# Two-layer graph network on one core: second-step products moved ahead of the attention, last normalization spread over other engines

## The chip, the core and the metric

The kernel runs on one core of a Trainium2 chip (trn2). The core has a matrix engine (TensorE; PE in the profile, with PEld for its weight loads), VectorE (DVE), ScalarE (ACT), GpSimd (POOL), and SyncE (SP), which here only issues DMAs. Each engine runs its own instructions in order and waits for the others through semaphores. Matrix products land in PSUM, everything else lies in SBUF or in DRAM. The metric is the device time of one execution in microseconds; the time before is the median of 3 runs.

## What is computed

Layer 0 is a graph attention layer with four heads over 4096 nodes; the change doesn't touch it. Layer 1 works on X = relu(layernorm(x)), 4096 rows of 256, in f32:

```
R = (S + I) / row sums                  # S: the adjacency matrix
Z = 0; Xf = X; Xa = X
for n in range(2):
    A  = top_p_attention(Xa)            # softmax of q k^T, cut to the top 90%, divided by its row sums
    Xf = R @ Xf
    Xa = A @ Xa
    Z  = Z + Xf @ U1[n].T + Xa @ U2[n].T
h = X + Z
out = x + (layernorm(h) * ln_g + ln_b)
```

q and k are products of Xa with 64-wide weights. The two parts that matter here are `Xa @ U2[n].T` and the closing layernorm.

## The kernel before

The 4096 rows are 32 blocks of 128 rows (P = 128, NB = 32). Layer 0 runs until about 830 us. Then each of the two steps has the same stages.

**A hop with the keys.** `hops` forms R @ Xf (line 601), 256 pieces of 4 products each, streaming the adjacency matrix from DRAM. It is a generator; between its pieces the kernel takes one item of `fills` and one of `picks`, two further generators. `fills` begins with `projections`: for each group g of 4 blocks it transposes 4 blocks of `cur` (line 732) into `xs`, multiplies xs with the merged key and query weights (line 738), and transposes the result into kT and qT (line 743). Each `yield` in `projections` is a place where the hop goes on. `fills` and `picks` then do the logits, exponentials and cuts of blocks 0 to 2. R @ Xf leaves in transposed form to `xft_d`, in step 0 also by rows to `xf_d`. In step 1 `cur` is loaded from `xa_d`, where step 0 left A @ Xa.

**The blocks.** For b = 0 to 31, `chosen_kept(b)` places the work of VectorE and GpSimd, and `attend` that of TensorE and ScalarE. In program order `chosen_kept(b)` has: `candidates(b)` (VectorE, many MAX8), `finish_scale(b-3)`, `first_step(b+2)` (some twenty small GpSimd instructions, lines 885 to 914, which end in the bound c), `third_probe(b+1)` (VectorE, one pass of 4096 columns, line 929, needs c), `finish(b-2)`, `finish_rows(b-3)`, and `masked(b)` (VectorE, one pass, line 972, gives the cut matrix e and its scale). `attend(b)` then works on block b while it makes the logits and exponentials of block b+3, called `ahead`:

- `start(c)`: a logits group, 4 products (line 701), and its exponentials on ScalarE (line 861), for c = 0 to 3
- `turn(g)`: 4 transposes of e (line 1035) into one of two PSUM tiles `tp`, and a copy to `eT` on ScalarE (line 1037); `gather(g)`: 4 products of eT with cur into `acc` (line 1043), g = 0 to 7
- `contribute(before)` and `contributed(before)`: for the block before, the row block xa is transposed (line 1055), copied to `zT` (line 1057), and multiplied with U2; the block's R @ Xf, `xf`, is multiplied with U1 (all four products in line 1063)
- `summed` and `first_probe` on ScalarE (lines 874 to 879 and 868), two passes per half of e
- `scaled`: A @ Xa out of acc, times the row scale (line 1047), to `xa_d` in step 0

So the order on TensorE at the start of a block is: logits 0, transposes of the block before's xa, turn 0, logits 1, turn 1, four products with U1 and U2, gather 0, logits 2, and so on. In the last three blocks of a step there is no block ahead and so no logits. In block 30, `looked` counts rows to be repaired (a small product, line 829, after the last cut); the repair itself stands in a branch behind each step.

**The end of a block.** `finish` adds the U1 part times rinv, the U2 part and, in step 0, X, in step 1 the partial sum z; step 0 stores to `z_d`, step 1 takes mean and variance (lines 148, 149). In step 1 `finish_scale` adds ln_b to x1 (line 1226) and computes 1/sqrt(variance + eps) on GpSimd (lines 1228, 1229), `finish_rows` does three VectorE passes of 256 columns (1233 to 1235) and SyncE stores the rows (1236).

**Weights.** `weights(n)` asks for U1[n] and U2[n] on SyncE's queue after the hop (line 691). `l1e` is a pool of four large tiles (tag e1), which hold the matrices e of the blocks and, in `projections`, kq and xs.

The order of calls is written out by hand (`manual_schedule`); each engine keeps it.

Of the kernel before, what the change touches and what calls it, by code (L numbers as in the profile page):

```python
# [26 lines left out]
P = 128  # L27
# [29 lines left out]
def gat_then_top_p_diffusion(  # L57
# [57 lines left out]
    z_d = dram.tile([NB, P, D], F32, name="z_d")  # L115
    x1_d = dram.tile([NB, P, D], F32, name="x1_d")
# [569 lines left out]
    def weights(n):  # L686

        both = l1.tile([P, 2, KC, D], F32, name="u")
        S.u = [both[:, i] for i in range(2)]
        for t, u in zip(S.u, (u1_t, u2_t)):  # L690
            nc.sync.dma_start(t, u[n].rearrange("(k p) m -> p k m", p=P))
# [23 lines left out]
    def projections(cur, n, G):  # L715
# [10 lines left out]
        lengths = small.tile([P, NB, 2], F32, name="lengths", bufs=1)  # L726
        for g in range(NB // 4):
# [6 lines left out]
            yield from waits(1 + n)  # L734
            pm = ps2.tile([P, 2, 512], F32, name="mm")
# [5 lines left out]
            yield from waits(1 + n)  # L741
# [9 lines left out]
            yield from waits(1 + n)  # L751
# [96 lines left out]
    def began(n, b, G):  # L848
# [6 lines left out]
        r.sums = small.tile([P, 2, 4], F32, name="sums", bufs=6)  # L855
        return r
# [166 lines left out]
    def loads(r):  # L1023
        r.xf, r.part = rows.tile([P, KC, P], F32, name="xf"), rows.tile([P, D], F32, name="part", bufs=3)
        nc.sync.dma_start(r.xf, xft_d[r.n][ds(r.b, 1)].rearrange("o p s i -> (o p) s i"))
        if r.n > 0:
            nc.sync.dma_start(r.part, block(z_d, r.b))
            r.x1 = rows.tile([P, D], F32, name="x1", bufs=3)
            nc.sync.dma_start(r.x1, block(x1_d, r.b))
        r.acc = ps1.tile([P, 2, D], F32, name="acc")  # L1030

# [13 lines left out]
    def scaled(r):  # L1045
        r.xa = rows.tile([P, D], F32, name="xa")
        nc.scalar.activation(r.xa, r.acc[:, 0, :], AF.Copy, scale=r.scale)
        if r.n + 1 < STEPS:
            nc.sync.dma_start(block(xa_d, r.b), r.xa)

    def contribute(r):

        pt = ps2.tile([P, 4, P], F32, name="tp")
        for k in range(KC):
            nc.tensor.transpose(pt[:, k, :], r.xa[:, ts(k, P)], ident)
        zT = rows.tile([P, 4, P], F32, name="eT", bufs=3)
        nc.scalar.copy(zT[:, :KC], pt[:, :KC])  # L1057
        return zT

    def contributed(r, zT):  # L1060
        for i, t in ((1, r.xf), (0, zT)):
            for k in range(KC):
                nc.tensor.matmul(r.acc[:, i, :], t[:, k, :], S.u[1 - i][:, k, :], start=(k == 0), stop=(k == KC - 1))  # L1063

    def attend(r, cur, before, ahead, between={}, eT=()):
# [8 lines left out]
        zT = contribute(before) if before else None  # L1074
        loads(r)
        eT = list(eT) or [turn(r, 0)]
        start(1)
        for g in range(NB // 4):
            if g + 1 < NB // 4:
                eT.append(turn(r, g + 1))  # L1080
            if g == 0 and before:
                contributed(before, zT)
            gather(r, eT[g], g, cur)
            if g < 2:
# [5 lines left out]
            if g in between:  # L1090
                between[g]()
        scaled(r)
# [85 lines left out]
    def completed(R, cur):  # L1178
# [6 lines left out]
        if r.n + 1 < STEPS:  # L1185
            r.x = rows.tile([P, D], F32, name="a_x", tag="xa")
            nc.vector.tensor_copy(r.x, X[:, ds(dve, 1), :].rearrange("p o d -> p (o d)"))
# [6 lines left out]
        contributed(r, contribute(r))  # L1194
        finish(r)
        finish_scale(r)
        finish_rows(r)
# [12 lines left out]
    def finish(r):  # L1210

        if r.n + 1 < STEPS:
            row, ri = (r.x, r.ri) if hasattr(r, "x") else (X[:, r.b, :], rinv[:, r.b:r.b + 1])
            nc.vector.scalar_tensor_tensor(r.part, r.acc[:, 1, :], ri, row, ALU.mult, ALU.add)
            nc.vector.tensor_add(r.part, r.acc[:, 0, :], r.part)
            nc.sync.dma_start(block(z_d, r.b), r.part)
        else:
            ri = r.ri if hasattr(r, "ri") else rinv[:, r.b:r.b + 1]
# [177 lines left out]
```

## Time and profile before

| | |
|---|---|
| median of 3 runs | 2915.61 us (2913.66 to 2918.56) |
| the profiled execution | 2918.28 us; its span 2916.5 us |
| granted TensorE clock, mean | 0.988 |
| hop of step 1 with the second keys | about 1866 to 2168 us |
| blocks of step 1 | about 2168 to 2906 us |
| VectorE busy, 1170 to 1840 us (step 0) | 575.80 of 670 us |
| VectorE busy, 2215 to 2880 us (step 1) | 636.38 of 665 us |
| ScalarE busy in the same stretches | 500.82 and 482.91 us |
| GpSimd busy in the same stretches | 194.30 and 308.63 us |
| products of line 1063 | 512 instructions, 131.6 us busy |
| transposes of line 1055 | 128 instructions, 24.8 us busy |

A row of the profile's groups names line, engine, operation, and the tiles as out<-in. PE MATMUL times are modelled and overlap, so the distance between the starts of successive instructions says more than the duration of one. An f32 product appears as two instructions. In a timeline each row is one run of like instructions: start, length, engine, line, and in brackets the idle time before it with what ended it.

### The profile page before, as it was taken

What the parts mean: (1) busy time and instruction counts of PE and PEld (TensorE: products, weight loads), DVE (VectorE), ACT (ScalarE), POOL (GpSimd) and SP (SyncE); (2) the same over time, 40 slices, a digit from 0 to 9 for tenths busy, and PEclk for the clock granted to TensorE, in tenths of its full rate; (3) what the DMA queues carried; (4) which work ended last, traced back from release to release, by engine and by line L of the source; (5) the groups of instructions that cost most, each with busy time, mean ns of one, the idle gap of its engine ahead of it and who ended that gap; (6) DMA issues with size and microseconds to landing.
All of it is one profiled execution on the core that took longest, in us unless ns stands there. A gap on an engine that the chain in (4) does not pass through costs nothing. (4 is left out here: it accounts for less than half of the span.)

```text
span 2916.5 us, 51977 instructions
## 1 busy us (share of the span) xinstructions
PE 2828.3 (97%) x19033; PEld 2475.8 (85%) x19033; DVE 2196.8 (75%) x5193; ACT 1908.9 (65%) x3063; POOL 763.6 (26%) x1661
## 2 busy tenths in 40 slices
PE   6899999999999999999999999999999999999998
PEld 4799999999977778888888888788778888888887
DVE  7776878778654384788888888442747999999996
ACT  6786787768633735777777776235337777777772
POOL 6501211111010210233322222000103444444442
PEclk8899999999999999999999999999999999999999
DMA  7969577695465784000000000488970000000000
GB/s 178 220 244 219 194 218 189 231 201 205 157 196 166 248 299 135 20 24 22 20 20 20 20 20 21 153 270 280 337 268 22 25 25 25 25 25 30 29 23 22
DMA packets 181148, 368.12 MB, mean 126 GB/s; under 512 B 17168, under 2 KB 133904, under 8 KB 176784
## 3 DMA queue, kind: packets, MB, share of 16 engines
q1 hardware_dynamic: 142352, 270.92, 28.2%
q0 software_dynamic: 21504, 83.89, 12.1%
q10 hardware_dynamic: 17024, 9.85, 1.1%
q8 instruction: 154, 2.52, 0.4%
q14 instruction: 114, 0.93, 0.1%
HBM read 301.35 MB, written 109.38 MB: 141 GB/s over the span
## 5 line engine op out<-in xcount | busy, mean ns | idle before, releaser
L1043 PE MATMUL acc<-X,eT 128*128 128x256 f32 x4096 | 966.0, 381 | 0.1
L1043 PEld LDWEIGHTS acc<-X,eT 128*128 128x128 f32 x4096 | 743.2, 190 | 97.7 <-ACT eT L1037 14.9
L391 PE MATMUL acc<-ut,m 128*128 128x195 bf16 (+1 forms) x8192 | 700.9, 247 | 8.2 <-DVE st L408 5.6
L391 PEld LDWEIGHTS <-m 128*128 128x128 fp8e4 x8192 | 696.4, 97 | 13.2 <-DVE st L408 4.7
L861 ACT ACTIVATE e<-mm,nm 128x1024 f32<-128x1024 f32 x256 | 287.0, 1121 | 311.0 <-PE mm L701 295.7
L365 ACT ACTIVATE g<-sr,d_big 128x1024 uint8<-128x1024 f32 x444 | 467.7, 1139 | 2.6 <-DVE m L371 2.6
L929 DVE SCALAR_TENSOR_TENSOR big<-e,c 128x4096 f32<-128x4096 f32 x58 | 273.0, 4707 | 121.2 <-POOL c L914 84.4
L1037 ACT COPY eT<-tp 128x512 f32<-128x512 f32 x512 | 299.6, 585 | 98.3 <-PE tp L1035 97.9
L885 POOL TENSOR_TENSOR sums<-sums 128x2 f32<-128x2 f32 x64 | 12.5, 196 | 1309.0 <-ACT void L868 1309.0
L947 DVE MAX8 cand<-big 128x8 f32<-128x228 f32 (+1 forms) x1152 | 348.3, 380 | 0.0
L601 PE MATMUL mm<-ar,hl 128*128 128x512 f32 x844 | 336.3, 401 | 10.8 <-DMA ar<-adj_d 2.9
L601 PE MATMUL acc<-ar,hl 128*128 128x512 f32 x844 | 329.4, 393 | 1.5 <-DVE ar L588 1.4
L1035 PE MATMUL tp<-ident,e 128*128 128x128 f32 x2048 | 310.5, 274 | 2.7 <-ACT eT L1057 0.3
L1035 PEld LDWEIGHTS tp<-ident,e 128*128 128x128 f32 x2048 | 248.7, 141 | 70.9 <-ACT eT L1057 28.4
L371 DVE TENSOR_TENSOR m<-g,ax 128x512 uint32<-128x512 uint32 x256 | 182.2, 712 | 115.5 <-PE acc L391 96.3
L972 DVE SCALAR_TENSOR_TENSOR e<-e,found 128x4096 f32<-128x4096 f32 x58 | 259.6, 4476 | 0.0
L868 ACT ACTIVATE void<-e,c1x 128x2048 int8<-128x2048 f32 x128 | 257.4, 2011 | 2.8 <-issue 2.0
L868 ACT ACTIVATE void<-e,c 128x2048 int8<-128x2048 f32 x128 | 257.4, 2011 | 0.0
L701 PE MATMUL mm<-kT,qT 128*128 128x512 f32 x512 | 197.6, 467 | 3.6 <-ACT e L861 2.2
L601 PEld LDWEIGHTS mm<-ar,hl 128*128 128x128 f32 x844 | 159.4, 189 | 48.6 <-issue 5.9
L372 DVE TENSOR_TENSOR m<-m,ax 128x512 uint32<-128x512 uint32 x256 | 177.7, 694 | 26.0 <-DVE m L371 0.9
L601 PEld LDWEIGHTS acc<-ar,hl 128*128 128x128 f32 x844 | 159.6, 189 | 34.5 <-DVE ar L588 2.6
(297 smaller groups left out, 3494.6 us busy)
## 6 DMA issues: line engine op xcount, KB each, us to landing
ar<-adj_d SPq DMA_DIRECT2D x211, 512.0 KB, 4.7
adj_d<-ax POOLq DMA_DIRECT2D x32, 2048.0 KB, 6.9
ut<-uv_d SPq DMA_DIRECT2D x60, 784.0 KB, 5.4
aru<-adj_d SPq DMA_DIRECT2D x45, 512.0 KB, 4.6
ax<-in_adj_t_dram POOLq DMA_DIRECT2D x32, 512.0 KB, 15.7
x<-xf_d SPq DMA_DIRECT2D x78, 128.0 KB, 5.1
xf<-xft_d SPq DMA_DIRECT2D x64, 128.0 KB, 2.2
sr<-s_d SPq DMA_DIRECT2D x15, 512.0 KB, 4.7
```

The costliest lines, as they stand in the source:

```text
L365: nc.scalar.activation(g[:, c, :], shared[k].sr, AF.Relu, scale=BIG, bias=d_big[:, h, j:j + 1])
L391: nc.tensor.matmul(shared[k].acc[i][:, t, :cols], m[t][:, c, ts(i, P)], shared[k].ut[j // QUARTER][:, j % QUARTER, t, :cols], start=(j == ...
L601: nc.tensor.matmul(A.acc[c][s], A.hl[m][:, t, ts(s, P)], A.ar[m][:, ts(c, 512)], start=(j == 0 and t == 0), stop=(j == NB - 1 and t == 1))
L701: nc.tensor.matmul(pm[:, h, :], q[t], kT[:, ds(h * (N // 2) + c * 512, 512)], start=(t == 0), stop=(t == 1))
L861: nc.scalar.activation(ev[:, :, c, :], r.pm[c], AF.Exp, bias=r.nm, accum_out=r.sums[:, c // 2, c % 2:c % 2 + 1])
L868: nc.scalar.activation(void, r.e[:, ts(h, N // 2)], (AF.Relu, AF.Sign)[i], bias=r.c1, scale=-1.0, accum_out=r.sums[:, h, 2 + i:3 + i])
L929: nc.vector.scalar_tensor_tensor(big, r.e, r.c3, r.e, ALU.is_le, ALU.mult, accum_out=r.low3)
L947: nc.vector.max(cand[:, s, :], big[:, edges[s]:edges[s + 1]])
L972: nc.vector.scalar_tensor_tensor(r.e, r.e, r.t, r.e, ALU.is_ge, ALU.mult, accum_out=kept)
L1035: nc.tensor.transpose(pt[:, i, :], r.e[:, ts(4 * g + i, P)], ident)
L1037: nc.scalar.copy(eT, pt)
L1043: nc.tensor.matmul(r.acc[:, 0, :], eT[:, i, :], cur[:, j, :], start=(j == 0), stop=(j == NB - 1))
```

## The change

- In step 1 `carried` multiplies each block's rows of Xa, while the keys are made, with U2 of both steps side by side (one product 512 wide for each half of the 256 inputs). The half for U2[0] is stored to a new DRAM tensor `v_d`; the half for U2[1] replaces the block's rows in `cur`. Since A @ (Xa @ U2.T) is (A @ Xa) @ U2.T, `gather` of step 1 then yields the U2[1] part itself.
- `contribute` is gone, and `contributed` holds only the two U1 products, at the end of the block's own `attend` (in block 31 of step 1 after gather 4, into a bank of its own).
- `weighed` copies that product, times rinv, to SBUF on ScalarE; `gathered` adds z, v and ln_b on GpSimd; `finish` of step 1 becomes one VectorE pass and the moments; `normal` (ScalarE) and `polished` (GpSimd) replace the three VectorE passes for all but the last two blocks, where `finish_rows` has two passes.
- In `chosen_kept` the GpSimd order is now polished(b-3), finish_scale(b-2), first_step(b+2), gathered(b-1).
- U2 is asked for in the last block of step 0 (`both_weights`, a tile of pool l1e), U1 after the hop as before.

```diff
+    def both_weights():
+        u2 = l1e.tile([P, N + NB], F32, name="u2", tag="e1")[:, :KC * STEPS * D].rearrange("p (k n m) -> p k n m", k=KC, n=STEPS)
+        for i in range(STEPS):
+            nc.sync.dma_start(u2[:, :, i, :], u2_t[i].rearrange("(k p) m -> p k m", p=P))
+        S.u2 = [u2]
...
+        def carried(xs, g, i):
+            if n == 0:
+                return
+            b = 4 * g + i
+            pt = ps2.tile([P, 4, P], F32, name="tp").rearrange("p a b -> p (a b)")
+            for k in range(KC):
+                nc.tensor.matmul(pt, xs[:, k, i, :], u2[:, k].rearrange("p n m -> p (n m)"), start=(k == 0), stop=(k == KC - 1))
+            v = rows.tile([P, D], F32, name="part", bufs=3)
+            nc.scalar.copy(v, pt[:, :D])
+            nc.scalar.dma_start(block(v_d, b), v)
+            nc.vector.tensor_copy(cur[:, b, :], pt[:, D:])
...
             yield from waits(1 + n)
+            carried(xs, g, 0)
             pm = ps2.tile([P, 2, 512], F32, name="mm")
...
-            yield from waits(1 + n)
+            yield
+            carried(xs, g, 1)
+            yield from waits(n)
...
-            yield from waits(1 + n)
+            yield
+            carried(xs, g, 2)
+            yield from waits(n)
+            carried(xs, g, 3)
+            if n > 0:
+                yield
...
     def scaled(r):
-        r.xa = rows.tile([P, D], F32, name="xa")
-        nc.scalar.activation(r.xa, r.acc[:, 0, :], AF.Copy, scale=r.scale)
         if r.n + 1 < STEPS:
...
-    def contributed(r, zT):
-        for i, t in ((1, r.xf), (0, zT)):
-            for k in range(KC):
-                nc.tensor.matmul(r.acc[:, i, :], t[:, k, :], S.u[1 - i][:, k, :], start=(k == 0), stop=(k == KC - 1))
+    def contributed(r):
+        for k in range(KC):
+            nc.tensor.matmul(r.far, r.xf[:, k, :], S.u1[:, k, :], start=(k == 0), stop=(k == KC - 1))
+
+    def weighed(r):
+        if r.n + 1 == STEPS:
+            nc.scalar.activation(r.xf.rearrange("p k i -> p (k i)"), r.far, AF.Copy, scale=r.ri)
+
+    def gathered(r):
+        if r.n + 1 == STEPS:
+            nc.gpsimd.tensor_tensor(r.part, r.part, r.v, ALU.add)
+            nc.gpsimd.tensor_tensor(r.x1, r.x1, ln_b_r, ALU.add)
+            nc.gpsimd.tensor_tensor(r.part, r.part, r.xf.rearrange("p k i -> p (k i)"), ALU.add)
...
+        if not last:
+            contributed(r)
+            weighed(r)
         scaled(r)
...
         else:
-            ri = r.ri if hasattr(r, "ri") else rinv[:, r.b:r.b + 1]
-            nc.vector.scalar_tensor_tensor(r.part, r.acc[:, 1, :], ri, r.part, ALU.mult, ALU.add)
-            nc.vector.tensor_add(r.part, r.acc[:, 0, :], r.part)
+            nc.vector.scalar_tensor_tensor(r.part, r.acc[:, 0, :], r.scale, r.part, ALU.mult, ALU.add)
...
+    def normal(r):
+        if r.n + 1 == STEPS:
+            nc.scalar.activation(r.part, r.part, AF.Identity, scale=r.rs, bias=r.nmr)
+
+    def polished(r):
+        if r.n + 1 == STEPS:
+            nc.gpsimd.tensor_tensor(r.part, r.part, ln_g_r, ALU.mult)
+            nc.gpsimd.tensor_tensor(r.part, r.part, r.x1, ALU.add)
+            nc.sync.dma_start(block(out.rearrange("(b p) d -> b p d", p=P), r.b), r.part)
...
                 if b > 2:
-                    finish_scale(blocks[b - 3])
-                if b + 2 < NB and not hasattr(blocks[b + 2], "stepped"):
-                    first_step(blocks[b + 2])
+                    polished(blocks.pop(b - 3))
...
                 if b > 1:
                     finish(blocks[b - 2])
-                if b > 2:
-                    finish_rows(blocks.pop(b - 3))
+                    finish_scale(blocks[b - 2])
+                if b + 2 < NB and not hasattr(blocks[b + 2], "stepped"):
+                    first_step(blocks[b + 2])
+                if 0 < b < NB - 1:
+                    gathered(blocks[b - 1])
                 if not hasattr(r, "kept"):
                     masked(r)
+                if 1 < b < NB - 1:
+                    normal(blocks[b - 2])
```

## The prediction

> **What bounds the kernel now.** I read the page first: its busy row and its chain of waits.
>
> ```profile
> PE 2828.3 (97%) x19033; PEld 2475.8 (85%) x19033; DVE 2196.8 (75%) x5193; ACT 1908.9 (65%) x3063; POOL 763.6 (26%) x1661
> ...
> PE acc L1043 12%; PE mm L701 4%; PE acc L601 3%; PE mm L601 3%; PE tp L1035 3%; ACT void L868 2%; PE acc L1063 2%; DVE e L972 0%; DMA X<-xa_d 0%; DMA ar<-adj_d 0%; PE mm L738 0%; ACT eT L1037 0%; DVE cand L947 0%; ACT e L861 0%; PE tp L732 0%
> ```
>
> TensorE leads the chain, but 97% is an average over stages. So I cut the span into stretches. The change touches three: the blocks of step 0 (about 1123 to 1862 us), the second hop with the second keys (1866 to 2168), and the blocks of step 1 (2168 to 2906). For the hop I asked for stretches of 20 us (columns: busy us with counts for PE, PEld, DVE, ACT, POOL; granted clock; DMA share; GB/s):
>
> ```profile
> 1900.00:1920.00 20.00, 19.84 (x120) 17.29 (x120) 11.01 (x20) 8.34 (x19) 0.00 (x0) 1.00 0.93 307
> 1920.00:1940.00 20.00, 20.00 (x125) 17.56 (x124) 10.00 (x19) 6.92 (x15) 0.00 (x0) 1.00 0.92 304
> ```
>
> While the keys are made PE has no gap to fill: work added there is paid in full, and the loads (DMA 0.93) only become more relaxed. For the blocks I read the timeline where one block ends and the next begins (step 0):
>
> ```profile
> 1402.93 0.41 PEld L701 LDWEIGHTS mm<-kT,qT 128*128 128x128 f32 x2
> ...
> 1403.87 0.33 PEld L1055 LDWEIGHTS tp<-ident,xa 128*128 128x128 f32 x2
> ...
> 1404.32 1.12 ACT L861 ACTIVATE e<-mm,nm 128x1024 f32<-128x1024 f32 x1 [0.50 <-PE mm L701]
> ...
> 1405.42 0.36 ACT L1057 COPY eT<-tp 128x256 f32<-128x256 f32 x1
> ...
> 1405.68 0.60 ACT L1037 COPY eT<-tp 128x512 f32<-128x512 f32 x1
> 1405.84 0.42 PEld L1035 LDWEIGHTS tp<-ident,e 128*128 128x128 f32 x4 [0.48 <-ACT eT L1057]
> ...
> 1406.23 0.73 PEld L1063 LDWEIGHTS acc<-u,xf 128*128 128x128 f32 x4
> ...
> 1406.99 0.84 PEld L1063 LDWEIGHTS acc<-u,eT 128*128 128x128 f32 x4
> ...
> 1407.85 1.70 PEld L1043 LDWEIGHTS acc<-X,eT 128*128 128x128 f32 x8
> ```
>
> I call 1402.93 the join, J: the last gather is out and the next block's work starts. The first gather starts at J+4.92 (1407.85). Between them lie two logits groups, two turns, the two transposes of L1055, the four products of L1063, and one stall of 0.48 us, for which the copy L1057 is named. A block lasts 23.35 us in both steps (the chain's x16 gather pieces in step 1 stand at 2466.08, 2489.43, 2512.77).
>
> **Part 1, the joins.** The change takes L1055, L1057 and the U2 half of L1063 away, and puts the two U1 products at the block's end, before the next logits. Removing 0.33 + 0.86 + 0.48 would suggest 1.6 us, but the transposes behind L1055 and behind the stall run in 0.43 and 0.42 us against 0.55 elsewhere. I therefore add up PE's new order by starts: U1 products 0.86, logits 0.94, turn 0.55, logits 0.77, turn 0.55 = J+3.67. That is a gain of 1.25 if nothing else is late. What is late next is ACT: in the trace the exponentials (L861) start 1.39 us after their logits' weights, the next copy can start 1.10 later, and the copy L1037 takes 0.60. The logits now start at J+0.86, so the first eT is there at 0.86 + 1.39 + 1.10 + 0.60 = J+3.95, and the gather starts at J+4.00. PE waits 0.33 us in a new place and the join gains 0.92 us. In step 1 ACT also gets L1047's successor (weighed, 0.48) once the U1 products are out, and one normal (about 0.41, as the 128x256 casts of L578): both end near J+2.1, just ahead of the exponentials at J+2.25. After the first gather nothing of PE's and ACT's order changes. There are 31 joins in each of 2 steps: 62 x 0.92 = **57 us gained**. The last three joins of a step have no logits and would gain 1.3 to 1.6, but there the totals of L829 wait for VectorE (PE already waits 1.5 us at 2881.8), so I leave them at 0.92.
>
> **Part 2, the products with both U2.** carried() adds, for each of 32 blocks of step 1, two products of 128x512 in f32. Each f32 product is two instructions (4096 of L1043 for 2048 products). No f32 product of that width is in the trace. By width the nearest row is L601 (f32r, one every 0.23 us); by type it is the gather, 256 wide:
>
> ```profile
> 2900.08 1.89 PE L1043 MATMUL acc<-X,eT 128*128 128x256 f32 x8
> ...
> 2902.25 3.62 PE L1043 MATMUL acc<-X,eT 128*128 128x256 f32 x16
> ```
>
> Eight more instructions take 1.73 us: 0.216 each for 256 columns. The Trainium skill (TensorE: Matmul & The Clock Gate, Back-to-back issue gap) gives N/2.4 + 2.5 ns, so 109 ns for 256 columns and 216 ns for 512. The row is twice the rule: an f32 instruction streams at half the pace, and I double with the width. By the rule the part would cost 32 x 4 x 0.216 = 28 us, by the row 32 x 4 x 0.43 = **55 us added**. I take the row, since its type is the same; 28 stays as the lower end. Above, change-overs and a late tile could add some 4 us. The two evacuations of each (ACT 0.37, DVE 0.42) and the store on ACT's queue lie under PE: ACT is busy 7 to 8 and DVE 10 to 11 of 20 us there. If that cover failed, carried() would wait for its PSUM tile, of which there are two. The eight more pauses in the generator shift the later picks by 8 of 256 pieces, about 9 us; the last pick ended at 2146, 22 us before the hop did. The early request of U2 is worth nothing: nothing waits for L690 now.
>
> **Part 3, ends.** At the end of step 0 the hop's products wait from 1861.28 to 1864.05 (2.77 us) for the last contribution; only the U1 products, 0.86, remain: 1.9 gained. At the very end the last gather's weights are in at 2905.46 and the last VectorE instruction ends at 2912.58, 7.1 later. New: acc is read 0.45 later (0.48), statistics 0.46 and 0.27, POOL 0.22 + 0.09 + 0.56 with the first fused pass beside it, last pass 0.43, plus some 0.4 because the two share a port: 3.4. That is **3.7 gained**.
>
> **Part 4, normalization.** In step 1 VectorE loses L1220 (0.45 from start to start) and three passes for which ACT and POOL stand in (1.22): its round, 23.23 us now (2499.84 to 2523.07, no gap), falls to 21.56. GpSimd gets three additions after first_step (gathered), two before it (polished) and one small instruction, less one addition: about 0.73 us each. Now the rule that speaks against it: the skill (SBUF — State Buffer, the single rule of the shared port pair) says a VectorE instruction with two SBUF inputs and a GpSimd instruction that reads SBUF exclude each other, whoever is second being fully blocked. The timeline agrees:
>
> ```profile
> 2499.77 0.73 POOL L1226 TENSOR_TENSOR x<-x,ln_b_r 128x256 f32<-128x256 f32 x1
> ...
> 2499.84 4.94 DVE L929 SCALAR_TENSOR_TENSOR big<-e,c 128x4096 f32<-128x4096 f32 x1 [0.16 <-POOL c L911]
> ...
> 2500.59 4.27 POOL L1228 TENSOR_SCALAR rs<-mv 128x1 f32<-128x1 f32 x1
> ```
>
> L929 took 4.94 instead of 4.49 us behind an addition, and a 0.2 us instruction took 4.27 behind L929. By the rule alone a blocked VectorE pass loses the whole 0.73, by the row 0.46; I use 0.46. If VectorE starts L929 the moment c is ready (J+7.2), one gathered addition passes with it (in the 21.56), two wait for its end and hold up finish: 1.46; polished hits L972: 0.46. That makes 23.5, more than the new block of 22.43. But then VectorE falls behind TensorE, c no longer releases L929, and the additions run ahead of it; 1.5 us behind, the round is about 22.0. There is room: L972 ends at J+19.3 now, near J+20 then, and the turn needs it at J+24. The other new waits also fit: SP's store of the output now waits for POOL's polished at about J+15, where it is issued today (2507.57), so swapped and loads behind it keep their time; normal in ACT's queue needs finish_scale by J+24 with the exponentials behind it, and finish_scale comes near J+21; first_step behind finish_scale on POOL is wanted at J+22.8. I cost this part at nothing.
>
> **Sum.** -57 + 55 - 1.9 - 3.7 = -7.6 us. The profiled execution took 2918.28 (span 2916.5 and 1.8 around it) and would take 2910.7; it lay 2.7 above the median of the three runs, 2915.61. Forecast: **2908 us**.
>
> **Rivals.** (A) The sum as above, chance 0.45, 2902 to 2913. (B) More is gained, chance 0.30: the wide product costs less than doubled (down to 28 us: 2881), or eT is not late at the join (62 x 1.25 = 78 gained: 2888). For it: the widths were extrapolated. Against: the f32 rows all pace at two cycles a column, and ACT's chain is read from the trace. (C) Slower, chance 0.13: the shared port makes VectorE the bound of step 1. It decides once contention costs more than 22.43 - 21.1 = 1.3 us a block at any lag; at 23.5 us a block, 28 blocks lose 1.07 each, 30 us: 2938. For it: L1228's 4.27 us. Against: the lag heals it. (D) Chance 0.12: PE in the hop also waits for carried's tiles, 0.1 to 0.4 us each, 3 to 13 us: 2911 to 2921. That the work merely moves from the blocks to the hop without effect lies between A and D.
>
> **Chances and range.** A measurement of this kernel can tell about 0.2%, 5.8 us: faster means below 2909.8. A gives 0.31 faster and 0.14 same; B 0.30 faster; C 0.09 slower, 0.04 same; D 0.07 same, 0.05 slower. That is 0.61, 0.25, 0.14. The range runs from B's 2884 to D's 2921 and leaves out most of C.
>
> **What would show it.** Joins: the time from the end of the last gather to the first gather falls from 4.92 to 4.0, with a wait of 0.3 for eT (L1037's copy) and a block of 22.4 in both steps. Hop: the new row 128x512 f32 x128 at 0.43 us apart, and a hop some 55 us longer. Step 1: POOL rows of 4 us beside L929 and L972, VectorE full, but no PE wait on L972. I am wrong if blocks of step 1 are longer than those of step 0 (C), if the products pace at 0.22 (B), or if PE waits on tp tiles in the hop (D).

## The result and the profile after

| | before | after |
|---|---|---|
| median | 2915.61 us (2913.66 to 2918.56) | 2897.87 us (2896.88 to 2900.28) |
| ratio | | 0.9941, 95% interval 0.9928 to 0.9954 |
| profiled execution, its span | 2918.28, 2916.5 us | 2899.5, 2897.7 us |
| block of step 0, of step 1 (first gather to first gather) | 23.35, 23.35 us | 22.31, 22.25 us |
| last gather's end to first gather, regular joins | 4.96, 4.96 us | 4.02, 3.97 us |
| first gather to first gather of the last block: step 0, step 1 | 719.2, 718.2 us | 686.2, 687.2 us |
| hop with the second keys: step 0's last gather to step 1's first | 309.6 us | 357.0 us |
| first gather of step 1's last block to the end | 27.5 us | 25.1 us |

The change made the kernel 17.7 us faster; 2908 was forecast. In the rows below, line numbers are those of the changed kernel: gather L1075 (was L1043), logits L707 (L701), turn L1067 and its copy L1069 (L1035, L1037), exponentials L890 (L861), third probe L958 (L929), masked L1001 (L972), hop products L602 (L601), U1 products L1085, products with both U2 L741.

The page of the changed kernel, its busy row, its chain of waits, and two of its groups:

```profile
PE 2814.0 (97%) x18777; PEld 2443.1 (84%) x18777; DVE 2171.2 (75%) x5069; ACT 1914.8 (66%) x3061; POOL 878.6 (30%) x1815
...
DVE 18%; PE 11%; issue 5%; DMA 2%; ACT 1%; POOL 0%; SPq 0%; ACTq 0%; DVEq 0%; POOLq 0%
...
L1085 PE MATMUL acc<-u,xf 128*128 128x256 f32 x252 | 64.9, 380 | 0.4
...
L741 PE MATMUL tp<-u,xs 128*128 128x512 f32 x128 | 60.5, 595 | 0.0
```

The chain now names VectorE ahead of TensorE. That invites the reading that VectorE has become the bound; the experiments below say otherwise.

The timeline of the changed kernel at a join of step 0 (start, length, engine, line; in brackets the idle time and what ended it):

```profile
1413.40 0.84 PEld L1085 LDWEIGHTS acc<-u,xf 128*128 128x128 f32 x4
...
1414.26 0.41 PEld L707 LDWEIGHTS mm<-kT,qT 128*128 128x128 f32 x2
...
1415.66 1.12 ACT L890 ACTIVATE e<-mm,nm 128x1024 f32<-128x1024 f32 x1 [0.52 <-PE mm L707]
...
1416.77 0.57 ACT L1069 COPY eT<-tp 128x512 f32<-128x512 f32 x1
...
1417.39 1.59 PEld L1075 LDWEIGHTS acc<-X,eT 128*128 128x128 f32 x8 [0.25 <-ACT eT L1069]
```

J is 1413.40. The logits start at J+0.86, the exponentials 1.40 later, the copy 1.11 after those, and the gather at J+3.99, as soon as the copy is out. Each term is the one that the forecast had; the wait for eT is 0.25 where 0.33 was said. The gather's weight loads take 1.59; before they took 1.70.

The products with both U2, in TensorE's timeline of the hop:

```profile
1903.13 0.42 PEld L741 LDWEIGHTS tp<-u,xs 128*128 128x128 f32 x2
1903.79 0.19 PEld L741 LDWEIGHTS tp<-u,xs 128*128 128x128 f32 x1 [0.24 <-issue]
1904.21 0.19 PEld L741 LDWEIGHTS tp<-u,xs 128*128 128x128 f32 x1 [0.24 <-issue]
1904.64 0.19 PEld L602 LDWEIGHTS mm<-ar,hl 128*128 128x128 f32 x1 [0.24 <-issue]
```

The last three starts stand 0.42 to 0.43 apart: an f32 instruction of 512 columns takes 0.43 us, the value chosen in the forecast, and not the 0.216 that the forecast worked out from the Trainium skill (TensorE: Matmul & The Clock Gate, Back-to-back issue gap), whose formula is for an isolated product.

VectorE and GpSimd of the changed kernel in a steady block of step 1, in two timelines:

```profile
2501.17 0.31 DVE L983 MAX8 best<-cand 128x8 f32<-128x144 f32 x1
2501.52 0.68 DVE L988 TENSOR_TENSOR_SCAN cum<-best,cum,zero 128x48 f32<-128x48 f32 x1
2502.23 0.59 DVE L992 TENSOR_SCALAR drop<-cum 128x48 f32<-128x48 f32 x1
2502.85 0.79 DVE L993 CUSTOM_DVE_ANT_0 work<-drop,best 128x48 f32<-128x48 f32 x1
...
2504.04 4.48 DVE L958 SCALAR_TENSOR_TENSOR big<-e,c 128x4096 f32<-128x4096 f32 x1
...
2509.53 4.45 DVE L1001 SCALAR_TENSOR_TENSOR e<-e,found 128x4096 f32<-128x4096 f32 x1
```

```profile
2499.67 0.34 POOL L940 TENSOR_SCALAR c<-fell,c,up 128x1 f32<-128x1 f32 x1
...
2501.35 0.73 POOL L1095 TENSOR_TENSOR part<-part,xf 128x256 f32<-128x256 f32 x1
2502.03 0.74 POOL L1275 TENSOR_TENSOR part<-part,ln_g_r 128x256 f32<-128x256 f32 x1
2502.85 0.73 POOL L1276 TENSOR_TENSOR part<-part,x 128x256 f32<-128x256 f32 x1
2509.70 4.36 POOL L1263 TENSOR_SCALAR rs<-mv 128x1 f32<-128x1 f32 x1 [6.12 <-DVE mv L150]
```

The bound c is ready at 2500.0, but L958 starts 4.03 us later: VectorE is behind, and GpSimd's additions run ahead of L958, beside L988, L992 and L993, which take 0.68, 0.59 and 0.79 instead of 0.32, 0.19 and 0.27. L958 itself keeps its 4.48. No wait of TensorE in step 1 names VectorE before the step's last joins.

### The profile page after: what moved, and what is told of

Same layout as the page of the kernel before. It is cut to its first block, busy times and chain, and to the rows that moved or that the text cites. A ratio compares the mean times of both kernels' runs of the same rounds, so it can differ in the third digit from the quotient of the medians.

```text
span 2897.7 us, 51524 instructions
## 1 busy us (share of the span) xinstructions
PE 2814.0 (97%) x18777; PEld 2443.1 (84%) x18777; DVE 2171.2 (75%) x5069; ACT 1914.8 (66%) x3061; POOL 878.6 (30%) x1815
## 5 line engine op out<-in xcount | busy, mean ns | idle before, releaser
L1075 PE MATMUL acc<-X,eT 128*128 128x256 f32 x4096 | 973.7, 383 | 3.3 <-ACT eT L1069 2.8
L1075 PEld LDWEIGHTS acc<-X,eT 128*128 128x128 f32 x4096 | 739.0, 190 | 111.4 <-ACT eT L1069 31.4
L890 ACT ACTIVATE e<-mm,nm 128x1024 f32<-128x1024 f32 x256 | 286.1, 1118 | 205.5 <-PE mm L707 204.1
L1069 ACT COPY eT<-tp 128x512 f32<-128x512 f32 x512 | 296.4, 580 | 89.7 <-PE tp L1067 89.6
L602 PE MATMUL mm<-ar,hl 128*128 128x512 f32 x844 | 341.8, 408 | 9.2 <-DMA ar<-adj_d 3.6
L958 DVE SCALAR_TENSOR_TENSOR big<-e,c 128x4096 f32<-128x4096 f32 x58 | 261.9, 4515 | 98.1 <-POOL c L943 58.8
L602 PE MATMUL acc<-ar,hl 128*128 128x512 f32 x844 | 328.3, 392 | 2.2 <-DVE ar L589 2.1
L1067 PE MATMUL tp<-ident,e 128*128 128x128 f32 x2048 | 306.1, 272 | 0.8 <-DVE e L1001 0.8
L1067 PEld LDWEIGHTS tp<-ident,e 128*128 128x128 f32 x2048 | 255.0, 140 | 60.4 <-PE acc L1085 1.2
L1001 DVE SCALAR_TENSOR_TENSOR e<-e,found 128x4096 f32<-128x4096 f32 x58 | 259.1, 4468 | 0.0
L707 PE MATMUL mm<-kT,qT 128*128 128x512 f32 x512 | 198.3, 468 | 3.6 <-ACT e L890 2.2
L602 PEld LDWEIGHTS mm<-ar,hl 128*128 128x128 f32 x844 | 158.8, 188 | 49.5 <-issue 9.2
L602 PEld LDWEIGHTS acc<-ar,hl 128*128 128x128 f32 x844 | 158.8, 188 | 38.8 <-issue 4.1
## 6 DMA issues: line engine op xcount, KB each, us to landing
ax<-in_adj_t_dram POOLq DMA_DIRECT2D x32, 512.0 KB, 16.1
```

The costliest lines, as they stand in the source:

```text
L602: nc.tensor.matmul(A.acc[c][s], A.hl[m][:, t, ts(s, P)], A.ar[m][:, ts(c, 512)], start=(j == 0 and t == 0), stop=(j == NB - 1 and t == 1))
L707: nc.tensor.matmul(pm[:, h, :], q[t], kT[:, ds(h * (N // 2) + c * 512, 512)], start=(t == 0), stop=(t == 1))
L890: nc.scalar.activation(ev[:, :, c, :], r.pm[c], AF.Exp, bias=r.nm, accum_out=r.sums[:, c // 2, c % 2:c % 2 + 1])
L958: nc.vector.scalar_tensor_tensor(big, r.e, r.c3, r.e, ALU.is_le, ALU.mult, accum_out=r.low3)
L1001: nc.vector.scalar_tensor_tensor(r.e, r.e, r.t, r.e, ALU.is_ge, ALU.mult, accum_out=kept)
L1067: nc.tensor.transpose(pt[:, i, :], r.e[:, ts(4 * g + i, P)], ident)
```

## The experiments

The open points were four: what the products really cost and why the hop grew by less than they take; whether the eT wait is real and could be avoided; whether the normalization's move matters; and whether VectorE, which has no gap in step 1, is the bound.

**The products alone.** In e3 `carried` returns at once, in e2 it multiplies with U2[1] only.

```diff
         def carried(xs, g, i):
-            if n == 0:
-                return
+            return
```

> carried does nothing (the products with both U2, the copies out of them and the store of v are left out), its pauses stay, v is not loaded in step 1 and GpSimd adds ln_b in its place; all else stays. The hop lasted 309.6 us before the change and 357.0 after it, 47.4 more, though the product rows themselves take 1.71 a block with change-over, 54.7 us. Theory (the products cover some 6 to 7 us of waits for X<-xa_d and for tiles that TensorE had in the hop before; what was given back was waiting): the hop falls to 308 to 311 and waits of over 1 us ahead of the transposes for X<-xa_d come back; the kernel 2849 to 2852. Rival (the give-back comes from something else in the change, as the shorter end of step 0, the earlier weights or the pauses): the hop falls by the full 54 or more, to 300 to 303, 2841 to 2845.

```diff
-                nc.tensor.matmul(pt, xs[:, k, i, :], u2[:, k].rearrange("p n m -> p (n m)"), ...)
+                nc.tensor.matmul(pt[:, D:], xs[:, k, i, :], u2[:, k, 1, :], ...)
```

> carried multiplies with U2 of the second step alone: products of 128x256 in place of 128x512, v holds the wrong half (U2 of the first step is left out), all else stays. Theory (an f32 product streams at two cycles a column, 0.216 us for each instruction of 256 columns, 0.43 for 512): 128 instructions lose 0.216 each, 27.6 us; the hop goes from 357.0 to 329.4 if all else in it stays, the kernel to 2870; where waits for a transfer or a tile that the products had covered come back, up to 2875. Rival 1 (an instruction has a fixed price, change-over and tile wait, that does not depend on its width): 2890 to 2898. Rival 2 (half the pace[...]): 14 us, 2884.

Measured: e3 2845.74 us, ratio to before 0.9751 (0.9735 to 0.9767), hop 302.0. The products cost 357.0 - 302.0 = 55.0 us, the forecast's term (that it fits to the decimal is luck: two hops of one kernel differ by more, see e9), and my theory for e3 fell: no wait comes back when they go. e2: 2876.06, ratio 0.9859 (0.9843 to 0.9876), hop 332.0: half the width gives 25.0 back of 27.6. The products themselves now start 0.215 us apart. Ahead of six of the groups of transposes of the new states waits for VectorE's copy in `carried` now show, 0.8 to 0.9 us each and 5.0 in all, which the wide products had covered; they are more than the 2.6 that are missing. So the price is one of columns.

**Why the hop grew by 47.4 and not by 53.** e3's hop is 7.6 us shorter than before's, though it does nearly the same work; the forecast knew of 1.9. e7 is e3 with the old number of pauses, e9 the kernel before once more, e10 the changed kernel once more.

```diff
             carried(xs, g, 3)
-            if n > 0:
-                yield
```

> As e3 (carried does nothing; the products with U2, their copies and stores and v are left out), with six pauses of the generator for each group of four blocks, as before the change, in place of seven. e3's hop was 302.0 us, 7.6 shorter than before's 309.6, though it does the same work less the 0.9 of two transposes and of products with U2 and less a wait for ScalarE at the end of step 0. Theory (with the seventh pause the transposes of the keys no longer meet a late copy of VectorE and the waits for X<-xa_d are shorter): the hop is 304 to 306 here, with a wait of 1.4 ahead of the transposes of kq, the kernel 2848 to 2850. Rival (it comes from step 0's shorter end, from which everything behind is moved forward against the transfers, or from spread between runs): 301.5 to 302.5, 2844 to 2847.

> The kernel before, unchanged, for a second trace of its hop. The wait ahead of the first transposes of the new states (for X<-xa_d) was 3.38 us in its trace and 1.7 in that of the changed kernel, but 3.4 and 3.5 in two experiments. If this wait is spread between executions, it is anything from 1.5 to 3.5 here and the hop (309.6) moves with it by up to 2 us. If it belongs to the kernel before, it is 3.2 to 3.5 again. The wait of 1.55 ahead of the transposes of kq (seen again in e7 with six pauses) is here in either case.

> The changed kernel, unchanged, beside e6 on the same chip and for a second trace of its hop: 2896 to 2901, blocks of 22.31 and 22.25 again; the hop within 2 us of 357.0.

e7: 2848.11, ratio 0.9769 (0.9752 to 0.9785), hop 304.5, so the seventh pause is worth 2.5 us in these two traces. The largest wait that it takes away is the one ahead of the moments products, which multiply all the keys (the expectations call them transposes of kq); in TensorE's timeline of e7, and in before's:

```profile
1916.41 1.01 PEld L781 LDWEIGHTS mm<-e 128*64 128x64 f32 x16 [1.37 <-issue]
```

```profile
1953.20 1.01 PEld L756 LDWEIGHTS mm<-e 128*64 128x64 f32 x16 [1.36 <-issue]
```

It is the same wait to 0.01; e3 and the changed kernel have none of that size there. e9's hop took 306.2 where before's trace has 309.6, so 3.4 of the 7.6 is spread between executions of one kernel. The granted TensorE clock goes with it: in before's hop it stood at 0.5 in three stretches of 3.41 us, in e9's in none. The whole hop of before and of e9, in the columns of the forecast's stretches (the clock is the third figure from the end):

```profile
1861.30:2170.90 309.60, 296.33 (x1453) 242.59 (x1452) 154.88 (x393) 110.92 (x229) 20.50 (x51) 0.98 0.88 294
```

```profile
1859.00:2165.20 306.20, 292.41 (x1453) 238.63 (x1452) 154.45 (x393) 110.88 (x229) 20.50 (x51) 1.00 0.89 297
```

A slow stretch does not cost the same everywhere. The first transposes wait for the new states (X<-xa_d) and start 18.1 to 19.8 us after the last gather in every trace but e6's. A slow stretch ahead of them only shortens that wait: it is 2.84 to 3.65 us where no such stretch lies ahead of it, 1.35 to 2.38 behind 3.41 us at 0.5, and 0.17 behind 6.83 us (e1b), e6 left aside. In before the stretches lie in and behind the wait, where they cost. e3 and the changed kernel have the same single stretch, ahead of the wait, so their difference of 55.0 is free of it. e10 had 357.0 again and 2901.54 (ratio 0.9938, 0.9922 to 0.9955), just above the 2896 to 2901 expected. From e9: 306.2, less 2.3 for the end of step 0 (the first wait among the hop's products ends 4.5 us after the last gather instead of 6.8), less 2.5 for the pause, plus 55.0 makes 356.4; the trace has 357.0.

**The early request.** e6 asks for U2 behind the last block.

```diff
-                beside.update({1: both_weights, 2: lambda: begin(second, 4), ...})
-            attend(r, cur, None, beside)
+                beside.update({2: lambda: begin(second, 4), ...})
+            attend(r, cur, None, beside)
+            if n + 1 < STEPS:
+                both_weights()
```

> The changed kernel with U2 of both steps asked for when the last block of step 0 has been issued, behind the first loads of the second hop on SP's queue, in place of during that block. The prediction cost the early request at nothing. Theory: carried first needs U2 some 24 us after the last gather, the transfers of adj run at a DMA share of 0.5 to 0.9 by then, and the request is behind only a few of them: 2896 to 2901, and no wait of L741. Rival: U2 arrives late and delays the loads behind it, and TensorE waits 2 to 8 us at the first carried: 2900 to 2906.

2905.55, ratio 0.9954 (0.9938 to 0.9971), beside e10's 2901.54 on the same chip. The intervals of the ratios overlap; the trace decides. TensorE's timeline of e6 in the first pieces of the hop:

```profile
1842.67 0.29 PEld L602 LDWEIGHTS mm<-aru,hl 128*128 128x128 f32 x1 [5.68 <-issue]
```

The changed kernel waits 3.1 to 3.3 us here (both traces), e6 5.7, and its hop is 360.1, 3.1 longer. The wait stands ahead of a hop product, not of L741: `carried` is in time. Late are the hop's loads: U2's 512 KB stand ahead of block 31's store to `z_d` on SyncE's queue, which lands 7.6 us after the last gather instead of 4.7, and the next loads are asked for right behind that, at 8.5 instead of 5.6. The forecast priced the early request at nothing; it is worth about 3 us.

**The join.** e4 moves the U1 products into the next block's join, where TensorE had waited for eT; e8 puts them behind the second turn instead of ahead of it.

```diff
-    def attend(r, cur, ahead, between={}, eT=()):
+    def attend(r, cur, before, ahead, between={}, eT=()):
...
+            if g == 0 and before:
+                contributed(before)
             if g + 1 < NB // 4:
                 eT.append(turn(r, g + 1))
+            if g == 0 and before:
+                weighed(before)
+                gathered(before)
             gather(r, eT[g], g, cur)
...
-        if not last:
+        if r.b + 1 == NB and not last:
             contributed(r)
```

> The U1 products of a block are moved from the block's end into the next block's join, behind the second logits group and ahead of the second turn, so that the logits start at once when the last gather is out; weighed and gathered follow behind the second turn (GpSimd's order stays, ScalarE has weighed behind the second copy eT). The last block keeps its own. Theory (the join is bound by ScalarE's chain logits, exponentials, copy eT, which now starts 0.84 late because the U1 products run first, with TensorE's own order at 3.67 us next): eT is there at J + 3.1, TensorE's order ends at J + 3.6 to 3.7, the wait for eT is gone, and blocks of step 0 go from 22.31 to 21.95. In step 1 VectorE (21.5 busy a block) has 0.4 left, so blocks go from 22.25 to 21.9. 60 joins by 0.35 are 21 us: 2875 to 2882. Rival 1 (VectorE is already the bound of step 1): only step 0 gains, 10 us, 2886 to 2889, and TensorE waits in step 1 for VectorE. Rival 2 (the copy eT is not late, the 0.25 named in the profile is paid elsewhere): 2896 to 2899.

> As e4, but the U1 products stand behind the second turn, right ahead of the first gather, where they were before the change; the turn runs ahead of them. TensorE's order at the join has the same rows as in e4, so the time from the last gather's end to the first gather is 3.7 here too. Theory (the first gather pays some 0.1 us for what stands right ahead of it: its weight loads took 1.70 behind the products before the change and 1.59 behind a turn after it): blocks last 22.1 in place of e4's 22.01, 62 by 0.1 are 6 us, 2888 to 2892. Rival (the 0.1 was something else): as e4, 2882 to 2887.

e4: 2884.48, ratio 0.9882 (0.9866 to 0.9899), the best kernel of this study, 13 us below the changed one. Its timeline at a join of step 0:

```profile
1409.61 0.41 PEld L707 LDWEIGHTS mm<-kT,qT 128*128 128x128 f32 x2
...
1411.00 1.12 ACT L890 ACTIVATE e<-mm,nm 128x1024 f32<-128x1024 f32 x1 [0.50 <-PE mm L707]
...
1411.88 0.85 PEld L1085 LDWEIGHTS acc<-u,xf 128*128 128x128 f32 x4
...
1412.11 0.58 ACT L1069 COPY eT<-tp 128x512 f32<-128x512 f32 x1
...
1412.75 0.57 PEld L1067 LDWEIGHTS tp<-ident,e 128*128 128x128 f32 x4
...
1413.30 1.60 PEld L1075 LDWEIGHTS acc<-X,eT 128*128 128x128 f32 x8
```

The copy ends at J+3.08, and the gather starts at J+3.69 without a wait: TensorE's own order sets it. Blocks last 22.01 in **both** steps, so TensorE still binds step 1 (rival 1 of the expectation falls). The blocks give 8.5 us in step 0 and 7.6 in step 1, 16.1 of the 21 expected. Its trace has a hop longer by 3.4 (360.4), which is not the products' doing: the granted clock stood at 0.5 for 6.83 us from 17.7 us after the last gather on, nearly all of it behind the wait ahead of the first transposes, and e11 below, with the same products in the join and no such stretch, has a hop of 356.9.

e8: 2886.54, ratio 0.9893 (0.9876 to 0.9909), blocks 22.03, not 22.1. The join is 3.63, 0.09 shorter than e4's, and the gather behind the products 1.70, 0.10 longer. So the 0.1 is no price: part of the products' own time is booked in whatever stands behind them. To compare two orders, measure to the end of the first gather, not to its start.

**The normalization on VectorE.** e1 and e1b give the three passes and the weighed sum back to VectorE.

```diff
-            nc.gpsimd.tensor_tensor(r.part, r.part, r.xf..., ALU.add)
+            nc.vector.tensor_tensor(r.part, r.part, r.xf..., ALU.add)
...
-                    polished(blocks.pop(b - 3))
+                    finish_rows(blocks.pop(b - 3))
...
-            nc.vector.scalar_tensor_tensor(r.part, r.part, r.mv[:, 0, 0:1], ln_g_r, ALU.subtract, ALU.mult)
-            nc.vector.scalar_tensor_tensor(r.part, r.part, r.rs, r.x1, ALU.mult, ALU.add)
+            nc.vector.tensor_scalar(r.part, r.part, r.mv[:, 0, 0:1], r.rs, ALU.subtract, ALU.mult)
+            nc.vector.tensor_mul(r.part, r.part, ln_g_r)
+            nc.vector.tensor_add(r.part, r.part, r.x1)
```

> The changed kernel with the normalization of step 1 given back to VectorE: the weighed sum is added to part by VectorE, and normal and polished are replaced by three passes of VectorE in finish_rows (GpSimd keeps z + v and x1 + ln_b). All else stays. Theory (the move to ScalarE and GpSimd is what lets VectorE keep up with a block of 22.25 us): VectorE was busy 579.4 of 600 us in the steady part of step 1, some 21.5 us a block; four passes more of 0.43 us make 23.2, less some 0.2 to 0.4 for GpSimd passes that no longer collide. Blocks of step 1 then last 22.9 to 23.1, step 0 stays at 22.3: 28 blocks by 0.7 are 20 us, 2912 to 2922, and TensorE waits for VectorE's L972 (here under its new line) or the transposes behind it. Rival (VectorE has room, and the lag of 3.7 us absorbs the passes, or the GpSimd passes cost VectorE as much as its own): blocks of step 1 stay at 22.3, 2896 to 2901.

e1: 3261.38, ratio 1.1179 (1.1161 to 1.1198). Blocks of step 1 took 34.8 to 36.1 us for the most part. The waits of e1 between 2300 and 2700 us (engine, line, waited for: us in all, times, longest):

```profile
POOL rs L1263 <- DVE mv L150: 235.0, 11, 21.4
...
DVE part L1095 <- POOL part L1093: 133.7, 11, 12.9
...
PE tp L1067 <- DVE e L1001: 121.7, 11, 11.1
```

e1 measures the place of one instruction and not the question: VectorE's new addition (L1095, ahead of L1001) waits for GpSimd's z + v (L1093), which stands behind first_step in GpSimd's queue, and first_step waits for ScalarE's probes of a later block. That is 12 us of wait a block, and each block's TensorE waits in turn for L1001. Behind such waits TensorE was also granted less: 0.84 on average from 2300 to 2700 us, where the changed kernel has 1.00. e1b has the addition one block later, in `finish`.

```diff
         else:
+            nc.vector.tensor_tensor(r.part, r.part, r.xf..., ALU.add)
             nc.vector.scalar_tensor_tensor(r.part, r.acc[:, 0, :], r.scale, r.part, ALU.mult, ALU.add)
```

> As e1, the normalization of step 1 on VectorE, but the weighed sum is added in finish, one block later, where GpSimd's z + v has long been made, so that no VectorE instruction waits for GpSimd's row behind first_step. Theory (VectorE is what the move relieves): some 23.0 us of VectorE a block against 22.25 of TensorE; blocks of step 1 last 22.8 to 23.1, 15 to 24 us longer in all, 2912 to 2922, with TensorE waiting for e<-e,found. If GpSimd's passes cost VectorE as much as its own, blocks stay at 22.3, 2896 to 2901.

e1b: 2915.92, ratio 0.9998 (0.9989 to 1.0007), that of the kernel before. VectorE's timeline of e1b:

```profile
2696.29 4.48 DVE L1001 SCALAR_TENSOR_TENSOR e<-e,found 128x4096 f32<-128x4096 f32 x1
...
2717.80 0.38 DVE L1281 TENSOR_SCALAR part<-part,mv,rs 128x256 f32<-128x256 f32 x1
2718.22 0.43 DVE L1282 TENSOR_TENSOR part<-part,ln_g_r 128x256 f32<-128x256 f32 x1
2718.68 0.42 DVE L1283 TENSOR_TENSOR part<-part,x 128x256 f32<-128x256 f32 x1
2719.02 4.48 DVE L1001 SCALAR_TENSOR_TENSOR e<-e,found 128x4096 f32<-128x4096 f32 x1
```

From L1001 to L1001 it is 22.73, with no gap. For the first 13 blocks of step 1 the blocks stay near 22.3 while VectorE falls behind; then they take its 22.73. Among the waits of e1b between 2300 and 2700 us there is now one that the changed kernel does not have:

```profile
PE tp L1067 <- DVE e L1001: 4.8, 9, 0.8
```

Here VectorE is the bound. The move to ScalarE and GpSimd is worth 2915.9 - 2897.9 = 18 us (17 by the ratios), as much as the whole change.

**More for GpSimd, and GpSimd at another time.** e5 adds four GpSimd additions a block; e11 is e4 with `polished` ahead of first_step.

```diff
             nc.gpsimd.tensor_tensor(r.part, r.part, r.xf..., ALU.add)
+            for op in (ALU.add, ALU.subtract) * 2:
+                nc.gpsimd.tensor_tensor(r.part, r.part, ln_b_r, op)
```

> The changed kernel with four more GpSimd additions a block at the end of gathered in step 1 (ln_b added and taken off again, twice; the sum is the same). It prices a GpSimd pass of 0.73 us in VectorE's time. VectorE is busy 21.5 of 22.25 us a block, so it has 0.75 to give. By full exclusion (0.73 each) its round becomes 24.4: blocks of step 1 24.4, 60 us more, 2958. By the 0.46 of one collision in the trace of before 23.3: 30 us more, 2928. If the passes run while VectorE is in instructions of one SBUF input and cost it little (under 0.2 each), or when they run wholly beside its search, blocks stay at 22.3: 2896 to 2901. I expect the middle, 2915 to 2930.

```diff
-                if b > 2:
-                    polished(blocks.pop(b - 3))
...
                     finish_scale(blocks[b - 2])
+                if b > 2:
+                    polished(blocks.pop(b - 3))
```

> As e4, with polished (two GpSimd additions a block in step 1) moved behind finish_scale and ahead of first_step, so that it runs beside VectorE's MAX8 search (one SBUF input) and not beside the small instructions behind it. In the changed kernel and in e4 VectorE has no gap in step 1, yet TensorE has none either: I read it that VectorE's own work is 21.0 us a block, and the rest, 1.3 and 1.0, is GpSimd's additions stretching L988 to L994; VectorE falls some 4 us behind the release of L958 until the stretching fits TensorE's block. Theory: blocks stay at 22.0 (TensorE binds), the small instructions are stretched less or by the three additions of gathered alone, VectorE settles less far behind, and the last joins of step 1 and the tail, where TensorE waits for VectorE (5.07 for a join of 1.87), get 1 to 3 us shorter: 2881 to 2884. Rival: first_step ends 1.4 later, L958 or the logits behind it waits for it, and blocks get longer than 22.1: 2887 or more.

e5: 2921.84, ratio 1.0022 (1.0016 to 1.0029), blocks of step 1 23.08. Its timelines of GpSimd and of VectorE:

```profile
2514.68 4.90 POOL L1277 TENSOR_TENSOR part<-part,ln_g_r 128x256 f32<-128x256 f32 x1
2519.66 0.73 POOL L1278 TENSOR_TENSOR part<-part,x 128x256 f32<-128x256 f32 x1
2520.49 4.27 POOL L1265 TENSOR_SCALAR rs<-mv 128x1 f32<-128x1 f32 x1
```

```profile
2514.05 4.95 DVE L958 SCALAR_TENSOR_TENSOR big<-e,c 128x4096 f32<-128x4096 f32 x1
```

The fourth extra addition reaches into L958 (4.95 for 4.48), and polished then stands behind L958 for 4.90 us and the scale behind L1001 for 4.27. GpSimd, at 367 of 400 us busy, has no room left, `normal` on ScalarE waits 0.8 a block for nmr with the exponentials behind it, and TensorE's weight loads wait 1.3 a block for eT (21.9 in 17 blocks), 0.8 more than in the changed kernel (8.2 in 18). That is the whole of the longer block: the join grew from 3.96 to 4.79. VectorE has no gap in e5 either. The time lies in the range expected, 2915 to 2930, but TensorE's wait runs through ScalarE and GpSimd's queue, and not through VectorE as the expectation had it; which of the two alone would hold the block at 23.08 was not separated.

e11: 2884.93, ratio 0.9891 (0.9875 to 0.9908), as e4. Its VectorE runs 2.53 us behind c instead of 4.03, and the join before block 30 falls from 5.07 to 3.57, but the last period grows from 21.98 to 25.29, and the time is the same. That growth cannot be laid to the move. The last period was 22.54 in the changed kernel's first trace and 25.55 in its second (e10): in e10 and e11 the granted clock stood at 0.5 for 6.83 us, beginning in TensorE's wait for the last cut (which ends at L857); in the first trace and in e4 it was 1.00 there. The next gather and the U1 products behind that wait, in TensorE's timeline of the changed kernel's first trace and of e10:

```profile
2868.56 1.59 PEld L1075 LDWEIGHTS acc<-X,eT 128*128 128x128 f32 x8
2870.18 0.84 PEld L1085 LDWEIGHTS acc<-u,xf 128*128 128x128 f32 x4
```

```profile
2868.19 3.06 PEld L1075 LDWEIGHTS acc<-X,eT 128*128 128x128 f32 x8
2871.34 1.62 PEld L1085 LDWEIGHTS acc<-u,xf 128*128 128x128 f32 x4
```

So whether the move itself wins the 1.5 us at the join before block 30 stays open.

Put side by side, from the trace (means over 2300 to 2700 us; "stretch" is the excess of L988, L992, L993, L994, L958 and L1001 over 0.32, 0.19, 0.27, 0.19, 4.48 and 4.45; the first four as in e1b, where no addition meets them):

| step 1 | block | L958 behind c | L988, L992, L993, L994 | stretch | block less stretch |
|---|---|---|---|---|---|
| after | 22.25 | 4.03 | 0.66, 0.59, 0.77, 0.28 | 1.33 | 20.92 |
| e4 | 22.01 | 4.03 | 0.46, 0.59, 0.79, 0.19 | 1.06 | 20.95 |
| e8 | 22.03 | 4.32 | 0.86, 0.69, 0.33, 0.19 | 1.10 | 20.93 |
| e11 | 22.01 | 2.53 | 0.58, 0.58, 0.68, 0.19 | 1.06 | 20.95 |
| e5 | 23.08 | 4.76 | 0.32, 0.55, 0.79, 0.74 | 2.11 | 20.97 |

VectorE's own work is 20.9 to 21.0 in all five. What fills the rest up to the block is contention; in the first four kernels it follows TensorE's block to within 0.03 us. A VectorE without a gap was therefore no sign of the bound: in those four it is filled up with waiting inside its instructions. How it settles at just that filling was not separated.

## Why the prediction was near, and where its sizes were off

The working summed to -7.6 us; the traces have -18.8. The direction and the places of the two large parts were right; the sizes were off in both, and part of the distance is no merit or fault of the forecast, since before's trace has a hop that is 3.4 longer than that of e9; the result lies in the range, 4 us below case A's own and 10 above B's nearer figure.

- **Part 1, the joins: right, and under-sized.** "PE waits 0.33 us in a new place" is 0.25; joins went from 4.96 to 4.02 and 3.97. But the blocks gave 33.0 and 30.9, together 63.9 where 57 was said. The term ended at the first gather's start; the 0.11 by which that gather itself was longer behind L1063 (1.70, now 1.59) was outside it, and e8 shows that this is the products' own time. Over 56 regular joins that is 6 us. The joins themselves gave 2.5 more than 56 by 0.92. The last three periods gave 3.4 in step 0 and 0.4 in step 1, for 2.8 each in the sum, so 1.7 less: together the 7 that were missing. In e10 the same three periods of step 1 cost 2.6 in place of the 0.4, with the clock at 0.5 in the last.
- **Part 2, the products: right, 55.0 (e3).** The row of the same type, not the rule, was the one to trust, and e2 gives the width. That they would lengthen the hop by their full time, less only 1.9, was off by 5.7: the hop measured 47.4. About 2.5 is the added pause (e7), which the forecast mentioned only as a delay of the later picks; up to 3.4 is spread of before's hop (e9), with the clock; 0.4 more came from the end of step 0. Rival D did not come: TensorE waits for no tile of `carried`.
- **"The early request of U2 is worth nothing"** failed as a judgement: late, it costs 3.1 in the hop (e6), since it holds up the store and the hop's loads behind it.
- **Part 3, ends.** The tail gave 3.1 behind the last gather (3.7 said), and the U1 products that now stand inside the last block of step 1, 0.8, were forgotten.
- **Part 4, normalization: right for the wrong amount.** VectorE fell behind and the additions moved off L958, as argued, so C did not come. But the lag is 4.0 us, not 1.5, and the round is not "about 22.0": VectorE's own work is 21.0, and contention fills the rest of the block. And "I cost this part at nothing" hides that step 1's half of Part 1 hangs on it: without the move VectorE needs 22.73 and the kernel is where it was (e1b).
- **Rival B** had an eT that isn't late, 2888, as one branch. eT was late; e4 shows what is gained when the order is mended, 2884.5. Its other branch, a cheaper product, fell with e3.

## What to carry to other kernels

An engine without a gap, even one that leads the chain of waits, is not yet the bound: look whether its instructions are longer than the same ones elsewhere, and shorten the other engine to see whether the block follows. Before you explain a few microseconds between two traces, compare the granted clock in the same stretch: three such differences here went with it. When work is moved off a queue, price it against what the other parts of the change then ask of that engine, not against today's round. Put work that waits for nothing where the bounding engine waits for another (13 us here, from a few moved lines), and measure a changed order from end to end of the same instruction.

## What the hardware showed

- GpSimd's additions of 0.73 us stretch VectorE's L988, L992, L993 and L994 (0.19 to 0.32 become 0.55 to 0.86), among them TENSOR_SCALARs with a single SBUF input, but not MAX8 (0.31) and MATCH_REPLACE8 (0.29). In the other direction a GpSimd instruction of 0.2 or 0.7 us that meets a VectorE pass of 4096 columns takes 4.3 to 4.9. The Trainium skill (SBUF — State Buffer, Who interferes with whom, the single rule) has full exclusion, whoever starts second being blocked: GpSimd's rows agree, and VectorE's too but for size: L958 in e5 began with 0.67 us of the addition still to run and lost 0.47.
- VectorE and GpSimd found a steady distance: in the changed kernel the lag of L958 behind c went 0.03, 0.04, 2.05, 2.97, 3.77, 3.80, 3.81, 4.03 over the first eight and then stayed at 4.03 (within 0.01). That contention holds it there is not shown: e1b, in which no addition meets those small instructions, settles too, at 4.26, and c stands in GpSimd's queue behind a scale that itself waits for VectorE's moments (L1263, 6.1 us a block).
- An f32 matmul instruction takes 0.216 us for 256 columns and 0.43 for 512, both twice the time that the forecast worked out from the skill's page.
- Executions of one kernel differ with the granted TensorE clock, which stood at 0.5 in stretches of 3.41 or 6.83 us in the traces compared above. Under it eight weight loads of a gather took 3.06 us instead of 1.59. The hop of before took 309.6 and 306.2, though its blocks agreed to 0.3 in 719; the blocks of step 1 of the changed kernel took 687.2 and 690.0, though its hop agreed. A slow stretch costs nothing where TensorE waits behind it for something that comes later anyway.
